# The last expert layer of a two-layer decoder: the branch behind the gathers' issue, the last norm on VectorE, the second bias in the residual, the plain norms in one group

## Chip, core and metric

One NeuronCore of a Trainium2 chip. The metric is the device time of one execution of the whole program, in microseconds (us), as the median of several runs. TensorE is called PE, VectorE DVE, ScalarE ACT, GpSimd POOL and SyncE SP, as in the profile. PE multiplies into PSUM, DVE and ACT work elementwise, POOL does small elementwise work and issues the indirect DMAs (gathers and scatters), SP issues plain DMAs.

## What is computed

The reference is a decoder of two layers over 8 sequences of 256 tokens of 256 numbers. Each layer is attention, cross attention and a mixture of experts, each followed by a residual and a layer norm. The change touches the end of the second layer: its cross attention's last block, and its experts.

```
x = layernorm(x + cross_attention(x, ctx))            # second layer
probs = softmax(x @ gate_w.T)                         # 2048 tokens, 8 experts
top2_w, top2_idx = top_k(probs, 2)
keep = counts <= cap                                  # cap = 1.25 * 2048 / 8 = 320
h = silu(x_of_expert @ w1[e] + b1[e])
y = h @ w2[e] + b2[e]
out = layernorm(x + sum over kept experts of y * probability)
```

An expert that got more than 320 assignments is dropped as a whole. With the given data at most two experts are kept, and the kernel handles one kept expert by a short way; for more than two (a number the program reads at run time) a branch runs a general way, `all_experts`. In all runs here the branch is not entered: its body is jumped over.

## The kernel before

Activations live in SBUF as `x`, 16 chunks of 128 tokens; two chunks are a block `b`, 0 to 7. The order of PE, ACT, DVE and POOL is written out by hand: each stage is a list of steps with block offsets (`round_of`), and `run` records them. Only SP, and POOL in the expert stage, are ordered by the scheduler.

**Second cross attention (`xattn`, L657 to L791).** In round b the steps run for blocks around b: scores, weights, averages for b, projection and residual for b-1 (`settle`, L611), then the norm of b-2 (`norm`, L126: two ACT instructions), its transpose (`turn_batch`), its rows to DRAM for the later gathers (`store`, L967), router logits and ranking (`logits`, `rank`). Tokens that no kept expert takes need only the final norm of x itself: `plain` (L1192) takes moments of a block on DVE and POOL, `give` (L1196) normalizes it on ACT into a buffer, and SP sends it to `out`. In the rounds `plain` runs three blocks behind and `give` four. After the last round a second list (L774) finishes blocks 6 and 7.

`moments` (L110) is: two `bn_stats` and two `bn_aggr` on DVE, then on POOL (L120 to L123) variance plus epsilon, power -0.5, minus the mean, times the scale. The norm is then one ACT instruction per chunk with scale and bias.

**Experts (`ffn1`, L1423).** In this order:
1. `choose` (L1097): counts against the cap, the `first` kept expert, and two whole numbers `n` (which expert, how many).
2. `values_load` (L1435): every engine loads the count into a register, then `tc.If(n > 2)` (L1436): every engine branches over `all_experts`.
3. `slots` (L1116): DVE and PE work out the tokens of the expert in 3 slots of 128 (`tok`).
4. three gathers `own` of token rows (L1442, by `gather` L1222), POOL.
5. `weigh` (L1177): the tokens' probabilities, transposed on PE, copied by ACT, stored to DRAM by SP; three gathers `wts` from there (L1446).
6. PE loads the expert's number (L1447). Per slot one PSUM tile `sums[i]` with two halves; PE puts the biases b1 and b2 into them by products with a row of ones (L1453: six matmuls, twelve rows in the trace).
7. `plain` of blocks 6 and 7; the rows are transposed (`turned`, L1469, copied out by DVE), first product (L1461), SiLU on ACT (L1484), `give` of blocks 6 and 7 (four ACT instructions), transposes of h (copied out by ACT, L1471), second product (L1461).
8. Per slot (L1497 to L1501): y = second sum times weight plus own row, moments on DVE, rsqrt on POOL; then, in a second loop, the norm on DVE (L1505) and the scatter to `out` (L1506), which waits for all blocks' stores, since it overwrites rows of them.

Of the kernel before, what the change touches and what calls it, by code (L numbers as in the profile page):

```python
# [10 lines left out]
F32 = mybir.dt.float32  # L11
# [7 lines left out]
P = 128  # L19
# [23 lines left out]
def decoder_kernel(ctx: ExitStack, tc: tile.TileContext, a, out):  # L43
# [66 lines left out]
    def moments(b, y):  # L110

        st = small.tile([P, 2, 6], F32, tag="st2", name="st2")
        mv = small.tile([P, 2, 2], F32, tag="mv2", name="mv2")
        rs = small.tile([P, 2], F32, tag="rs2", name="rs2")
        nm = small.tile([P, 2], F32, tag="nm2", name="nm2")
        for c in range(2):
            nc.vector.bn_stats(st[:, c, :], y[:, c, :])
        for c in range(2):
            nc.vector.bn_aggr(mv[:, c, :], st[:, c, :])  # L119
        nc.gpsimd.tensor_scalar(rs, mv[:, :, 1], EPS, None, ALU.add)  # L120
        nc.gpsimd.tensor_tensor(rs, rs, mhalf[:, 0:2], ALU.pow)
        nc.gpsimd.tensor_scalar(nm, mv[:, :, 0], -1.0, None, ALU.mult)
        nc.gpsimd.tensor_tensor(nm, nm, rs, ALU.mult)  # L123
        waiting[b] = y, rs, nm

    def norm(b):  # L126
# [382 lines left out]
    class Steps:  # L509
# [101 lines left out]
        def settle(self, b):  # L611
            add_residual(b, self.py.pop(b), self.y.pop(b), self.bk)


    def xcontext(w, ctxT, es):
# [41 lines left out]
    def xattn(w, given, clamp, route, es):  # L657
# [50 lines left out]
        if clamp is None:  # L708
# [57 lines left out]
            (store, -2),  # L766
            (give, -4),
            (st.residual, 0),
# [3 lines left out]
            (rank, -2),  # L772
            (plain, -3),
        ], [  # L774
            (st.turn, B - 1),
            (st.project, B - 1),
            (st.settle, B - 1),
            (norm, B - 2),
            (turn_batch, B - 2),
            (store, B - 2),  # L780
            (logits, B - 2),
            (norm, B - 1),
            (turn_batch, B - 1),
            (store, B - 1),
            (give, B - 4),
            (rank, B - 2),
            (plain, B - 3),
            (logits, B - 1),
            (give, B - 3),
            (rank, B - 1),  # L790
# [136 lines left out]
    class Route:  # L927
# [169 lines left out]
        def choose(self):  # L1097


            p = ps.tile([P, 512], F32, tag="ps", name="p_cnt")  # L1100
            mm(p[:, 0:NE], [(onesb, self.acc[:, NC, :])])
            keep = self.keep = self.kept([NE], "keep")
            first = self.first = self.kept([NE], "first")
            prior = self.temp([NE, NE], "prior")
            n = self.temp([2], "n")
            self.n = self.kept([2], "ni", I32)
            nc.vector.tensor_scalar(keep, p[:, 0:NE], float(CAP), None, ALU.is_le)
            nc.vector.tensor_tensor(prior, tri, keep.unsqueeze(1).broadcast_to([P, NE, NE]), ALU.mult)
            nc.vector.tensor_reduce(first, prior, AX.X, ALU.add)
            nc.vector.scalar_tensor_tensor(first, first, 0.0, keep, ALU.is_equal, ALU.mult)  # L1110
            nc.vector.tensor_tensor(prior[:, 0, :], first, iota[:, 0:NE], ALU.mult)
            nc.vector.tensor_scalar(prior[:, 1, :], keep, 1.0 / NE, None, ALU.add)
            nc.vector.tensor_reduce(n, prior[:, 0:2, :], AX.X, ALU.add)
            nc.vector.tensor_copy(self.n, n)

        def slots(self):  # L1116
# [33 lines left out]
            for h in range(2):  # L1150
                oh = self.temp([NC // 2, P], "oh", BF16)
                shape = [P, NC // 2, P]
                nc.vector.tensor_tensor(  # L1153
                    oh, iotab.unsqueeze(1).broadcast_to(shape),
                    row[:, h * (NC // 2):(h + 1) * (NC // 2)].unsqueeze(2).broadcast_to(shape), ALU.is_equal,
                )
                for c in range(NC // 2):
                    nc.tensor.matmul(  # L1158
                        p[:, 0:2 * NS], oh[:, c, :], o2[:, h * (NC // 2) + c].rearrange("p i n -> p (i n)"),
                        start=(h + c == 0), stop=(h == 1 and c == NC // 2 - 1),  # L1160
                    )
            at = self.temp([NS], "at")
            tok = self.kept([NS], "tok", I32)
# [3 lines left out]

            to = self.kept([NS], "to", I32)
            none = self.temp([NS], "none")
# [4 lines left out]

            return tok, to, places

# [246 lines left out]
    def ffn1(r, b1, b2, b1r, w1, w2, ys, dump):  # L1423

        rows = r.rows.rearrange("c k p d -> (c k p) d")
        with ExitStack() as es:
# [7 lines left out]
            nc.scalar.activation(unused, r.lg[:, NC - 1, 0:1], AF.Silu)  # L1434
            n = nc.values_load(r.n[0:1, 1:2], min_val=1, max_val=NE)  # L1435
            with tc.If(n > 2):  # L1436
                all_experts(r, b1, b2, w1, w2, ys, dump, rows)
            tok, to, places = r.slots()
            own, wts = [], []
            for i in range(NS):  # L1440
                own.append(wk.tile([P, D], F32, tag="own", name="own"))
                gather(own[i], rows, tok[:, i:i + 1])  # L1442
            wrows = r.weigh()
            for i in range(NS):
                wts.append(wk.tile([P, 1], F32, tag="wts", name="wts"))
                gather(wts[i], wrows, tok[:, i:i + 1])  # L1446
            e = nc.tensor.value_load(r.n[0:1, 0:1], min_val=0, max_val=NE - 1)  # L1447

            sums = []
            for i in range(NS):  # L1450
                p = ps.tile([P, 2, D], F32, tag="ps", name="p_u")
                for k, b in ((0, b1r), (1, b2.rearrange("p e d -> p (e d)"))):
                    nc.tensor.matmul(  # L1453
                        p[:, k, :], ones[0:1, :], b[0:1, bass.ds(e * D, D)],
                        start=(k == 0), stop=False, skip_group_check=True,
                    )
                sums.append(p)

# [7 lines left out]
            def turned(t, name):  # L1466
                pt = ps.tile([P, 512], F32, tag="ps", name="pt_" + name)
                for f in range(2):
                    nc.tensor.transpose(pt[:, f * P:(f + 1) * P], t[:, f * P:(f + 1) * P], ident)  # L1469
                tT = wk.tile([P, 2, P], F32, tag=name + "T", name=name + "T")  # L1470
                (nc.scalar.copy if name == "h" else nc.vector.tensor_copy)(  # L1471
                    tT, pt[:, 0:2 * P].rearrange("p (k t) -> p k t", k=2)
                )
                return tT

            f1, f2 = (w.rearrange("p e c n -> p (e c n)") for w in (w1, w2))
            for b in range(B - 2, B):
                r.plain(b)
            xgT = [turned(own[i], "xg") for i in range(NS)]
            hs = []  # L1480
            for i in range(NS):
                into(0, i, xgT[i], f1)
                hs.append(wk.tile([P, D], F32, tag="h", name="h"))
                nc.scalar.activation(hs[i], sums[i][:, 0, :], AF.Silu)  # L1484
            for b in range(B - 2, B):
                r.give(b)
            hT = [turned(hs[i], "h") for i in range(NS)]
            for i in range(NS):
                into(1, i, hT[i], f2)
            places()  # L1490
            ends = []
            for i in range(NS):
                y = wk.tile([P, D], F32, tag="y1", name="y1")
                st = small.tile([P, 6], F32, tag="st1", name="st1")
                mv = small.tile([P, 2], F32, tag="mv1", name="mv1")
                rs = small.tile([P, 1], F32, tag="rs1", name="rs1")
                nc.vector.scalar_tensor_tensor(y, sums[i][:, 1, :], wts[i][:, 0:1], own[i], ALU.mult, ALU.add)  # L1497
                nc.vector.bn_stats(st, y)  # L1498
                nc.vector.bn_aggr(mv, st)
                nc.gpsimd.tensor_scalar(rs, mv[:, 1:2], EPS, None, ALU.add)  # L1500
                nc.gpsimd.tensor_tensor(rs, rs, mhalf[:, 0:1], ALU.pow)  # L1501
                ends.append((y, mv, rs))
            fixed = []
            for i, (y, mv, rs) in enumerate(ends):
                nc.vector.tensor_scalar(y, y, mv[:, 0:1], rs, ALU.subtract, ALU.mult)  # L1505
                s = nc.gpsimd.indirect_dma_start(  # L1506
                    out=out, out_offset=bass.IndirectOffsetOnAxis(ap=to[:, i:i + 1], axis=0), in_=y, in_offset=None,
                    bounds_check=NT - 1, oob_is_err=False,
                )
                after(s, r.given)  # L1510
                for other in fixed:
                    tc.declare_no_dep(s.ins, other.ins, reason="no two slots have one token")
                fixed.append(s)

    def after(s, others):
# [7 lines left out]
    def all_experts(r, b1, b2, w1, w2, ys, dump, rows):  # L1523

        with ExitStack() as es:
# [31 lines left out]
            for e in range(NE):  # L1557
                xg = wk.tile([P, 2, NS * P], F32, tag="xgT", name="xgT")
                for i in range(NS):
# [7 lines left out]
                    )  # L1567
                hT = wk.tile([P, 2, NS * P], F32, tag="hT", name="hT")
                for f in range(2):
# [9 lines left out]
            for b in range(B):  # L1579
                z = wk.tile([P, 4, D], F32, tag="z", name="z")  # L1580
                load_back(z, returned(ys, 2)[b], sent)
# [8 lines left out]
                nc.gpsimd.tensor_copy(x[:, 2 * b:2 * b + 2, :], y)  # L1590
            nc.vector.memset(r.first, 0.0)
            for b in range(B - 2):
                r.plain(b)
# [214 lines left out]
```

## Time and profile before

| what | value |
|---|---|
| runs | 1028.88, 1022.90, 1025.72 us; median 1025.72 |
| profiled execution | 1028.25 us; its span from first to last instruction 1026.5 us |
| mean granted PE clock | 0.952 of full |
| busy over the span | PE 927.8, DVE 568.3, ACT 494.4, POOL 296.0 us |

Busy time by stretch of the span (us), with the granted clock:

| stretch | PE | DVE | ACT | POOL | PE clock |
|---|---|---|---|---|---|
| 800 to 850 | 42.98 | 23.11 | 23.87 | 16.04 | 0.97 |
| 850 to 900 | 44.27 | 32.06 | 28.90 | 4.04 | 1.00 |
| 900 to 950 | 42.01 | 36.93 | 30.07 | 11.11 | 0.89 |
| 950 to 984 | 17.18 | 16.51 | 10.00 | 5.40 | 0.55 |
| 984 to 1027 | 18.52 | 13.54 | 4.17 | 14.17 | 0.58 |

How to read it: up to about 950 us PE works nearly without a gap. After that no engine is busy for more than about half of the time: the last block's chain and the experts' chain run from engine to engine, and what counts there is which wait ends last. In the views, a time is the start from the span's beginning and the next number the duration; a name such as `DVEq` is the engine's sequencer, which handles loads of registers, branches and waits.

### The profile page before, as it was taken

To read this page: it belongs to the slowest core of one execution; us is meant where nothing else is said; L and a number is where in the kernel's file an instruction comes from. 1 tells how busy PE (TensorE), PEld (TensorE's weight loads), DVE (VectorE), ACT (ScalarE), POOL (GpSimd) and SP (SyncE) were. 2 spreads that over 40 slices of the span, in tenths; PEclk is the share of its full clock that TensorE was granted. 3 is DMA by queue.
4 is the path that set the end of the run, shared out by engine and by line. 5 is a ranking of instruction groups with operands and counts; after the bars stand their busy time and mean duration, and the time that the engine had idled before them with its cause. 6 is when DMAs were issued, how large, how long until landed. Compare 5 with 4: busy or idle time off the path is not lost. (4 is left out here: it accounts for less than half of the span.)

```text
span 1026.5 us, 24279 instructions
## 1 busy us (share of the span) xinstructions
PE 927.8 (90%) x9877; PEld 623.3 (61%) x9877; DVE 568.3 (55%) x1480; ACT 494.4 (48%) x1055; POOL 296.0 (29%) x533
## 2 busy tenths in 40 slices
PE   8999999998999859999999999999999978888633
PEld 4677767765677546666666645666666556665522
DVE  3987776784577752222222246666665445776551
ACT  5677777745666422212222135555565545556211
POOL 3232222241211322333332133344433520112222
PEclk9999999999999969999999999999999999998556
DMA  8100000007211271222111030000000041001110
GB/s 233 14 3 3 3 3 3 3 10 267 75 42 43 56 225 49 67 67 66 58 42 42 21 113 22 22 22 1 2 1 1 2 158 59 15 29 42 39 32 29
DMA packets 45367, 50.97 MB, mean 50 GB/s; under 512 B 9854, under 2 KB 37806, under 8 KB 45249
## 3 DMA queue, kind: packets, MB, share of 16 engines
q1 hardware_dynamic: 37170, 36.37, 10.9%
q0 software_dynamic: 4256, 10.87, 3.7%
q10 hardware_dynamic: 3824, 2.10, 0.8%
q8 instruction: 82, 1.34, 0.6%
q14 instruction: 35, 0.29, 0.1%
HBM read 36.00 MB, written 13.51 MB: 48 GB/s over the span
## 5 line engine op out<-in xcount | busy, mean ns | idle before, releaser
L120 POOL TENSOR_SCALAR rs<-mv 128x2 f32<-128x2 f32 x48 | 15.2, 316 | 337.9 <-DVE mv L119 200.3
L852 DVE TENSOR_REDUCE m<-p_s 128x2 f32<-128x512 f32 x128 | 78.7, 683 | 50.2 <-PE p_s L846 50.2
L1382 DVE TENSOR_TENSOR h<-h,p_v 128x512 f32<-128x512 f32 x36 | 24.8, 688 | 109.6 <-PE p_v L1376 109.6
L870 ACT ACTIVATE e<-p_st 128x512 f32<-128x512 f32 x128 | 66.3, 618 | 30.0 <-PE p_st L553 30.0
L54 PE MATMUL p_pv<-e,vals 77*32 77x256 f32 (+1 forms) x1024 | 70.6, 396 | 11.3 <-DVE e L696 10.4
L1391 ACT COPY hT<-pt_h 128x512 f32<-128x512 f32 x36 | 21.1, 586 | 118.8 <-PE pt_h L1389 118.8
L689 ACT ACTIVATE e<-p_st 77x512 f32<-77x512 f32 x128 | 65.3, 591 | 21.7 <-PE p_st L553 21.7
L1228 POOL DMA_INDIRECT ys<-yo,dst x36 | 35.4, 985 | 135.6 <-DVE yo L1403 135.6
L1398 PE MATMUL p_y<-fw,hT 128*128 x288 | 68.1, 379 | 0.7 <-ACT hT L1391 0.7
L1398 PEld LDWEIGHTS p_y<-fw,hT 128*128 128x128 f32 x288 | 54.6, 190 | 23.3 <-issue 16.5
L1376 PE MATMUL p_u<-fw,xgT 128*128 x144 | 67.9, 594 | 0.4 <-DVE d L1347 0.4
L1376 PE MATMUL p_v<-fw,xgT 128*128 x144 | 67.7, 592 | 0.0
L873 POOL TENSOR_SCALAR_AFFINE_SELECT e<-e 128x256 f32<-128x256 f32 x128 | 49.9, 407 | 36.3 <-ACT e L870 31.9
L673 DVE TENSOR_REDUCE m<-p_s 128x4 f32<-128x308 f32 x128 | 52.1, 469 | 12.6 <-PE p_s L54 12.0
L54 PEld LDWEIGHTS p_pv<-e,vals 77*32 77x32 f32 (+1 forms) x1024 | 33.3, 111 | 38.4 <-issue 8.0
L562 ACT COPY u<-p_pv 128x512 f32<-128x512 f32 x48 | 28.2, 588 | 55.4 <-PE p_pv L54 55.3
L1376 PEld LDWEIGHTS p_v<-fw,xgT 128*128 128x128 f32 x144 | 27.4, 190 | 34.4 <-issue 34.4
L129 ACT ACTIVATE x<-y,nm,rs 128x256 f32<-128x256 f32 x64 | 34.9, 597 | 24.3 <-POOL nm L123 24.3
L1381 ACT ACTIVATE h<-p_u 128x512 f32<-128x512 f32 x36 | 21.5, 597 | 46.0 <-PE p_u L1376 36.5
L1222 POOL DMA_INDIRECT xg<-rows,tok x36 | 35.1, 975 | 28.8 <-DMA fw<-in_L_ffn_W 15.7
L863 PE MATMUL p_st<-qT,kT 32*128 32x256 f32 x512 | 41.9, 400 | 0.0
L375 POOL COPY aT<-s 32x128 f32<-32x128 f32 x32 | 9.3, 289 | 104.6 <-DVE s L371 103.9
(304 smaller groups left out, 2137.2 us busy)
## 6 DMA issues: line engine op xcount, KB each, us to landing
fw<-in_L_ffn_W SPq DMA_DIRECT2D x24, 512.0 KB, 6.7
rows<-x SPq DMA_DIRECT2D x24, 256.0 KB, 2.2
z<-ys SPq DMA_DIRECT2D x8, 512.0 KB, 3.8
m<-in_L_ffn_w SPq DMA_DIRECT2D x16, 256.0 KB, 5.1
x<-in_x SPq DMA_DIRECT2D x8, 256.0 KB, 7.8
out<-plain SPq DMA_DIRECT2D x8, 256.0 KB, 2.1
b<-in_L_ffn_b SPq DMA_DIRECT2D x8, 128.0 KB, 4.8
xg<-rows,tok POOLq DMA_INDIRECT x36, 2.8
```

The source lines that it names most:

```text
L54: nc.tensor.matmul(dst, l, r, start=(i == 0), stop=(i == n - 1))
L129: nc.scalar.activation(x[:, 2 * b + c, :], y[:, c, :], AF.Identity, bias=nm[:, c:c + 1], scale=rs[:, c:c + 1])
L673: nc.vector.tensor_reduce(st.less(b)[:, c, j, :], p, AX.X, ALU.max, negate=True)
L689: nc.scalar.activation(e[0:KV, i].rearrange("p i q -> p (i q)"), p[0:KV].rearrange("p i q -> p (i q)"), AF.Exp)
L852: nc.vector.tensor_reduce(st.less(b)[:, c, j, 2 * t:2 * t + 2], p, AX.X, ALU.max, negate=True)
L863: nc.tensor.matmul(tiles[j][:, i, :], kTs[b][r, t, i, c * P:(c + 1) * P], st.qT[b][r, t, :], start=(i == 0), stop=False, skip_group_check= ...
L870: nc.scalar.activation(e.rearrange("p i q -> p (i q)"), p.rearrange("p i q -> p (i q)"), AF.Exp)
L873: nc.gpsimd.affine_select(out=e[:, :, o], in_=e[:, :, o], compare_op=ALU.is_ge, fill=0.0, base=0, pattern=[[0, 2], [2 * c - 1, P]], channe ...
L1222: nc.gpsimd.indirect_dma_start(out=out, out_offset=None, in_=table, in_offset=bass.IndirectOffsetOnAxis(ap=index, axis=0),)
L1228: s = nc.gpsimd.indirect_dma_start(out=table, out_offset=bass.IndirectOffsetOnAxis(ap=index, axis=0), in_=rows, in_offset=None,)
L1376: nc.tensor.matmul(p, xg[:, dc, :], w[:, bass.ds(e * (2 * FF) + dc * FF, FF)], start=(dc == 0), stop=(dc == 1),)
L1398: nc.tensor.matmul(y, hT[:, f * P:(f + 1) * P], w3[:, bass.ds(e * (4 * D) + f * D, D)], start=(f == 0), stop=(f == 3),)
```

## The change

Seven things, all near the end:
- The last block's residual takes its moments at once (`settle_now`, with the new `statistics`), and its norm is done by DVE (`norm_now`) with the mean subtracted and the scale multiplied, so POOL has only the power left to do.
- In the rounds `plain` runs four blocks behind and `give` five; blocks 4 to 7 are left to the expert stage, where `statistics` takes the eight chunks' moments in one group.
- `values_load` and the branch stand behind the issue of all gathers, not ahead of `slots`. The two numbers are worked out in `numbers`, inside `slots`.
- Only b1 is put in by products. b2 is added to the own row on DVE (`own_b`), times the weight, ahead of the end.
- Blocks 4 to 7 are normalized one by one, block 4 on ACT, the others on DVE, each sent by a DMA of its own from four buffers.
- The copies of the transposed own rows go from DVE to ACT.
- At the end slots are interleaved: end(0), end(1), send(0), end(2), send(1), send(2). Variance plus epsilon is DVE's, the power POOL's.

In the jumped-over body, two tiles get fewer buffers, `at` is set to -1, and the statistics are taken again.

```diff
+    def statistics(y, pool, tag):
+        n = y.shape[1]
...
+        for c in range(n):
+            nc.vector.bn_stats(st[:, c, :], y[:, c, :])
+        for c in range(n):
+            nc.vector.bn_aggr(mv[:, c, :], st[:, c, :])
+        nc.vector.tensor_scalar(rs, mv[:, :, 1], EPS, None, ALU.add)
+        nc.gpsimd.tensor_tensor(rs, rs, mhalf[:, 0:1].broadcast_to([P, n]), ALU.pow)
+        return mv, rs
...
+        def settle_now(self, b):
+            y = self.bk.tile([P, 2, D], F32, tag="y2", name="y2")
+            nc.vector.tensor_tensor(y, self.py.pop(b), self.y.pop(b), ALU.add)
+            self.y[b] = y, *statistics(y, self.bk, "n")
+
+        def norm_now(self, b):
+            y, mv, rs = self.y.pop(b)
+            for c in range(2):
+                nc.vector.tensor_scalar(
+                    x[:, 2 * b + c, :], y[:, c, :], mv[:, c, 0:1], rs[:, c:c + 1], ALU.subtract, ALU.mult
+                )
...
-            (give, -4),
+            (give, -5),
...
-            (plain, -3),
+            (plain, -4),
         ], [
...
-            (st.settle, B - 1),
+            (st.settle_now, B - 1),
...
-            (norm, B - 1),
+            (st.norm_now, B - 1),
...
-            (give, B - 4),
             (rank, B - 2),
-            (plain, B - 3),
+            (give, B - 5),
             (logits, B - 1),
-            (give, B - 3),
             (rank, B - 1),
...
         def choose(self):
...
-            nc.vector.tensor_tensor(prior[:, 0, :], first, iota[:, 0:NE], ALU.mult)
-            nc.vector.tensor_scalar(prior[:, 1, :], keep, 1.0 / NE, None, ALU.add)
-            nc.vector.tensor_reduce(n, prior[:, 0:2, :], AX.X, ALU.add)
+        def numbers(self):
...
+            nc.vector.tensor_tensor(at[:, 0, :], self.first, iota[:, 0:NE], ALU.mult)
+            nc.vector.tensor_scalar(at[:, 1, :], self.keep, 1.0 / NE, None, ALU.add)
+            nc.vector.tensor_reduce(n, at, AX.X, ALU.add)
             nc.vector.tensor_copy(self.n, n)
...
+            self.numbers()
             at = self.temp([NS], "at")
...
-            n = nc.values_load(r.n[0:1, 1:2], min_val=1, max_val=NE)
-            with tc.If(n > 2):
-                all_experts(r, b1, b2, w1, w2, ys, dump, rows)
-            tok, to, places = r.slots()
+            tok, at, places = r.slots()
...
             wrows = r.weigh()
+            last = slice(2 * B - 8, 2 * B)
+            mv, rs = statistics(x[:, last, :], wk, "p")
             for i in range(NS):
                 wts.append(wk.tile([P, 1], F32, tag="wts", name="wts"))
                 gather(wts[i], wrows, tok[:, i:i + 1])
+            n = nc.values_load(r.n[0:1, 1:2], min_val=1, max_val=NE)
+            with tc.If(n > 2):
+                all_experts(r, b1, b2, w1, w2, ys, dump, rows)
...
+            places()
             e = nc.tensor.value_load(r.n[0:1, 0:1], min_val=0, max_val=NE - 1)
...
-                for k, b in ((0, b1r), (1, b2.rearrange("p e d -> p (e d)"))):
-                    nc.tensor.matmul(
-                        p[:, k, :], ones[0:1, :], b[0:1, bass.ds(e * D, D)],
-                        start=(k == 0), stop=False, skip_group_check=True,
-                    )
+                nc.tensor.matmul(
+                    p[:, 0, :], ones[0:1, :], b1r[0:1, bass.ds(e * D, D)], start=True, stop=False,
+                    skip_group_check=True,
+                )
...
+            def give(b, eng):
+                o = wk.tile([P, 2, D], F32, tag="plain", name="plain", bufs=4)
...
-                (nc.scalar.copy if name == "h" else nc.vector.tensor_copy)(
+                nc.scalar.copy(
...
-            for b in range(B - 2, B):
-                r.give(b)
+            for b in range(B - 4, B):
+                give(b, nc.scalar if b < B - 3 else nc.vector)
             hT = [turned(hs[i], "h") for i in range(NS)]
...
+            ev = nc.vector.value_load(r.n[0:1, 0:1], min_val=0, max_val=NE - 1)
             for i in range(NS):
...
+                nc.vector.scalar_tensor_tensor(
+                    t, b2.rearrange("p e d -> p (e d)")[:, bass.ds(ev * D, D)], wts[i][:, 0:1], own[i],
+                    ALU.mult, ALU.add,
+                )
+                own_b.append(t)
+            def end(i):
...
+                nc.vector.scalar_tensor_tensor(
+                    y[:, 0, :], sums[i][:, 1, :], wts[i][:, 0:1], own_b[i], ALU.mult, ALU.add
+                )
+                ends.append((y, *statistics(y, small, "e")))
+            def send(i):
...
+            for i in range(NS + 1):
+                if i < NS:
+                    end(i)
+                if i:
+                    send(i - 1)
```

## The prediction

> **What bounds the kernel now.** First the table by stretches: to 950 us PE is busy 42 to 44 of every 50 us, and the change puts nothing on PE there. So I read the last 75 us: the timeline, then the chain of work that ended last, then the rows of the branch's line. (Columns: start, duration.) The timeline of the last block's norm:
>
> ```profile
> 963.15 0.69 DVE L136 TENSOR_TENSOR y<-p_y,x 128x512 f32<-128x512 f32 x1 [1.65 <-PE p_y L54]
> ...
> 968.59 0.23 POOL L120 TENSOR_SCALAR rs<-mv 128x2 f32<-128x2 f32 x1
> 968.91 0.71 POOL L121 TENSOR_TENSOR rs<-rs,mhalf 128x2 f32<-128x2 f32 x1
> ...
> 970.22 1.09 ACT L129 ACTIVATE x<-y,nm,rs 128x256 f32<-128x256 f32 x2 [2.41 <-POOL nm L123]
> ...
> 974.64 0.17 DVE L985 TENSOR_REDUCE sm<-p_l 128x2 f32<-128x16 f32 x1 [3.25 <-PE p_l L54]
> ```
>
> To see: the residual is ready at 963.84, x only at 971.31. Between them DVE does a plain block's moments first and POOL that block's four small operations, so this block's start at 968.59. PE, DVE and ACT wait.
>
> The branch's line (ns min/median/max, first and last start):
>
> ```profile
> L1436 DVEq COMPARE_BRANCH  x1: 56/56/56, 980.3 to 980.3; - x1
> L1436 PEldq COMPARE_BRANCH  x1: 3583/3583/3583, 980.3 to 980.3; - x1
> L1436 POOLq INC_SWDGE_SEM  x1: 1797/1797/1797, 981.2 to 981.2; - x1
> L1436 DVEq EVENT_SEMAPHORE  x1: 21/21/21, 984.2 to 984.2; - x1
> ```
>
> To see: PE and DVE need 3.6 and 3.9 us to get over the jumped body; ACT and POOL get on at 980.7. And the chain behind it:
>
> ```profile
> 984.27 0.29 DVE own L1121
> ...
> 992.47 5.45 PE p_u L1453 x12
> 997.92 1.47 PE pt_xg L1469 x6
> 999.39 4.84 PE p_u L1461 x12
> ...
> 1005.03 0.59 ACT plain L1200
> ...
> 1006.11 0.49 ACT plain L1200
> ...
> 1006.91 3.58 PE p_u L1461 x8
> ...
> 1014.50 0.71 POOL out L1506
> ...
> 1017.20 0.97 POOL out L1506
> ```
>
> To see: bias products, transposes, first product, two blocks' norms on ACT in the way of hT, second product, and three scatters in a row. From the last scatter's start to the span's end are 9.3 us that the change doesn't touch.
>
> **The change, part by part**, all in times of this profile.
>
> *Last norm.* In the changed program's order DVE does, from the residual's end at 963.84, the rest of the previous ranking mixed with this block's moments: 0.41, 0.39, 0.42, 0.39, 0.18, twice 0.16, 0.19, 0.18 = 2.5 us, so epsilon is in at 966.3. POOL has the power alone (0.71, L121) and nothing ahead of it: 967.1. DVE norms the first chunk (0.4, as L1505), then one addition (0.19), two bn_stats of a plain block (0.74), one aggregate (0.16), then the second chunk (0.4): 969.0 against 971.31. **Gain 2.3.** What is late next: the previous blocks' ranking on DVE (967.84 to 970.52, 2.7 us) now runs 969.15 to 971.85, and the logits arrive at 974.64 - 2.3 = 972.3, so 0.5 us of cover. Ends: 0 (that cover gone and POOL slowed), 3.1 (the eight logit products take 1.06 us at 964.22 under clock 1.00, 1.88 at 972.73 under 0.50, if the shorter gap keeps the clock). I take 2.3, the direct sum.
>
> *Branch and second bias.* `first` ends at 979.15, and `slots` starts there instead of 984.27: 5.1 us earlier. The four instructions of `numbers` (0.66, L1111 to L1114) stand ahead of `at`, where DVE waited 0.47 for PE: 0.2 lost. So `tok` is there at 985.7, the own gathers go at 986.5, 987.9 and 989.1 (spacing 1.3 as before, the same 0.8 after `tok`), the last landing 3.2 us later (gathers' median), 992.3.
> But the branch now stands behind `statistics` on DVE: ws done at 986.5, eight bn_stats (0.37 each, L117 0.74 for two) and eight aggregates (0.15 each) = 4.2, epsilon 0.2: 990.7. Then 4.3 from the register's load to the event behind the jump (979.9 to 984.2): **995.0**. PE meets its own branch at 987.0, and 0.3 + 3.6 + 0.6 (load of the expert's number, 991.6 to 992.2) bring it to 991.5. There it stops: in the built program its first bias product (L1489 of the changed kernel) waits for a DVE count that lies past DVE's branch, since the jumped body uses the same PSUM buffers. Queued behind it are all products, and everything waits for those. From 995.0 three bias matmuls at 5.45/6 = 0.9 each end at 997.7, against 997.92. **Gain 0.2**: 5.1 + 2.7 us shorter work, of which DVE's 4.4 us of statistics and the later jump eat nearly all. Ends: gain 3.6 if DVE's jump costs nothing (PE from 991.5, end 994.3, the gathers there by 992.3); loss 1.0 if the jump's code comes 1.2 us later. I take 0.2, since DVE jumps over some 240 instructions where 230 cost 3.9.
> [...]
>
> *Elsewhere in that stage, at no cost.* POOL: power over eight columns, between 0.58 (one column) and 2.8 (four times two columns' 0.71), about 1.5; it delays the last weight gather to about 994.4, landing by 997; POOL leaves the branch after that and after 1.8 of INC_SWDGE_SEM, at 999, needed at 1009. DVE behind the jump: places 0.4, two nm 0.4, six norms 2.4, a register load 0.3, three own_b at 0.5: done by about 1001, needed at 1007.6. SP: four stores at 0.38; two stand in the queue behind the one that waits for ACT's block, so they go by 1006.9 and land at about 1009 (2.1 each), where the first scatter waits for them at 1011.4: cover 2.4, and without it what is over is lost. The copies of xg on ACT take 0.30 (L1471) for DVE's 0.43, hidden by PE's own transposes.
>
> *Plain norms on ACT.* Between h and hT stand two instructions instead of four, 2.06/4 = 0.51 each. **Gain 1.0**; ends 0.5 (a wait for the transposes instead, ending 1005.1) and 1.1.
>
> *End.* Second product shifted by 0.2 + 1.0: slot 0's y at 1007.6. Its residual 0.48, stats 0.43, aggregate 0.18, epsilon 0.17, with hand-offs 1009.0; power 0.58: 1009.7. Slot 1's row of four ends at 1010.7, then norm 0: 1011.0; POOL's second power 1011.36; first scatter 1011.45 (1.10). Slot 2 ends at 1012.4, but its power stands behind that scatter: 1012.85 to 1013.45. Second scatter 1013.5, third 1014.8 against 1017.20: 2.4, of which 1.2 are the shift. **Gain 1.2.** Ends 0 (POOL's gaps of 0.3 at each change) and 2.0 (no power between the scatters).
>
> *Rounds.* Each round keeps one plain and one give, one block later; the moved blocks' 1.1 us of ACT and 1.0 of DVE each leave a stage that PE bounds: 0, ends -0.5 and +1.0.
>
> Sum: 2.3 + 0.2 + 1.0 + 1.2 = 4.7. Against the profiled execution's own 1028.25 that is 1023.6. That execution is 2.5 above the median of the runs, so against the median of 1025.72: **1021.0**.
>
> **Rivals.**
> - *B, DVE's jump doesn't hold PE.* For: ACT's and POOL's jumps cost 0.4, and both fetches lay at one time before. Against: the 3.9 row. 3.4 more: 1017.6. Chance 0.10.
> - *C, the clock stays up.* In the rows by microsecond the granted clock is 0.50 from 997 to 1003, 1.00 from 1004 to 1007, 0.58 at 1007 and 0.50 to 1010, after the gap of 1005.1 to 1006.9. That gap shrinks by 1.0. At the factor 1.88/1.06 the second product's 4.54 would take 2.6: 2 more, 1019.0. Against: first product and bias may as well fall on other steps of the clock. Chance 0.12. [...]
> - *D, the norm's gain isn't there*: DVE's mixed order makes ranking late, or POOL's power is slowed by DVE. 1023.3. Chance 0.17.
> - *E, slower*: DVE's fetch at 991 now runs among the six gathers' packets (before, DMA moved little but instructions at 979 to 985, and 27 to 261 GB/s at 993 to 997), and nothing else covers it. Every us more is one of span; from 3.9 + 4.7 = 8.6 us on it is slower than before. At three times, 11.7: 1028.8. Against: the busy share of DMA at 993 to 997 is 0.25 to 0.47. Chance 0.06, mostly with a smaller loss.
> - The forecast itself: 0.55, alone 1018.8 to 1023.3.
>
> **The numbers.** A measurement tells about 0.5% (5.1 us) from no change. 1020.6 is that bound, close under the forecast: of the forecast 0.40 falls beyond, of B and C nearly all, of D none: 0.22 + 0.20 = 0.42 faster. Slower by over 0.5% is about half of E and a little for what I don't see: 0.05. The rest, 0.53, is within. The range runs from B's side, 1017.0, to D with the worse ends of the stores and of POOL's gaps, 1024.8; the runs' own spread of 1022.9 to 1028.88 is part of that.
>
> **What would show it.** Right: the last x normed by DVE about 2 us sooner; DVE's event behind the branch about 4 us after the load, PE's first bias product straight behind it; bias, transposes and products ending no more than some 0.3 us sooner counted from `first`; two ACT norms ahead of hT; scatters 1.3 to 2.1 apart. Wrong: PE's bias products before DVE's event; scatters waiting for the blocks' stores; a fetch of over 6 us.

## The result, and the profile after

The changed kernel takes 1016.16 us (median of 5 runs, 1014.33 to 1018.12); the kernel before, beside it, 1027.66 (5 runs): ratio 0.9895, 95% interval 0.9863 to 0.9927. A second set of runs gave 1017.41 (6 runs) against 1025.35 (19 runs): 0.9918, interval 0.9888 to 0.9948. Over all eleven runs the changed kernel's median is 1016.68; the kernel before has 1024.64 to 1025.35 in its four larger sets (12 to 22 runs). So the gain is **some 8.4 us (8.0 to 8.7), where 4.7 was forecast**: faster, as the forecast says, but by nearly twice as much, and the 1016.16 lies below the forecast's range (1017.0 to 1024.8).

The profiled execution (1016.16, span 1014.4) is 12.1 us shorter than that of before. About 3 of these are the first profile's bad luck: at 1028.25 it lay some 3 above the median of its kernel.

The last block's norm, in the timeline (start, duration):

```profile
959.04 0.69 DVE L631 TENSOR_TENSOR y<-p_y,x 128x512 f32<-128x512 f32 x1 [1.17 <-PE p_y L54]
...
960.64 0.42 DVE L133 BATCH_NORM_STATS2 st<-y 128x6 f32<-128x256 f32 x1
960.97 0.17 DVE L1039 TENSOR_SCALAR sel<-rk 128x32 bf16<-128x32 f32 x1
961.04 0.24 DVE L135 BATCH_NORM_AGGREGATE mv<-st 128x2 f32<-128x6 f32 x2
...
961.32 0.17 DVE L136 TENSOR_SCALAR rs<-mv 128x2 f32<-128x2 f32 x1
961.57 0.71 POOL L137 TENSOR_TENSOR rs<-rs,mhalf 128x2 f32<-128x2 f32 x1 [9.39 <-DVE rs L136]
...
963.46 0.38 DVE L637 TENSOR_SCALAR x<-y,mv,rs 128x256 f32<-128x256 f32 x1
...
967.17 0.18 DVE L1010 TENSOR_REDUCE sm<-p_l 128x2 f32<-128x16 f32 x1 [0.65 <-PE p_l L54]
```

To see: x is ready 4.11 after the residual's end (959.73 to 963.84), where it was 7.47. On DVE the second bn_stats is given as 0.42, but the next instruction starts 0.33 later, and the two aggregates together take 0.24.

The branch's line (ns min/median/max, first and last start):

```profile
L1477 PEldq COMPARE_BRANCH  x1: 3356/3356/3356, 979.4 to 979.4; - x1
...
L1477 DVEq COMPARE_BRANCH  x1: 56/56/56, 982.4 to 982.4; - x1
L1477 PEldq EVENT_SEMAPHORE  x1: 51/51/51, 982.8 to 982.8; - x1
...
L1477 DVEq EVENT_SEMAPHORE  x1: 21/21/21, 986.3 to 986.3; - x1
```

To see: PE is over the body at 982.8, DVE 3.9 after its own branch at 986.3. DVE branches later than PE because the statistics of eight chunks stand ahead: 2.70 for eight bn_stats from 978.75 on, 0.62 for eight aggregates from 981.37 on. The chain of waits (start, duration) goes on behind DVE's event:

```profile
986.60 2.90 PE p_u L1489 x6
...
995.51 1.08 ACT plain L1506 x2
...
996.90 1.15 PE p_u L1515 x4
...
1001.91 0.49 POOL out L1562
```

To see: PE's bias products start 0.3 behind DVE's event; one block's two norms stand ahead of hT. The three scatters start at 1001.91, 1003.75 and 1005.09.

### The profile page after: what moved, and what is told of

The parts are those of the page before. It is cut to its first block, busy times and chain, and to the rows that moved or that the text cites. A ratio compares the mean times of both kernels' runs of the same rounds, so it can differ in the third digit from the quotient of the medians.

```text
span 1014.4 us, 24247 instructions
## 1 busy us (share of the span) xinstructions
PE 919.8 (91%) x9871; PEld 617.2 (61%) x9871; DVE 571.0 (56%) x1495; ACT 491.2 (48%) x1050; POOL 289.0 (28%) x512
## 5 line engine op out<-in xcount | busy, mean ns | idle before, releaser
L54 PE MATMUL p_pv<-e,vals 77*32 77x256 f32 (+1 forms) x1024 | 68.0, 384 | 10.7 <-DVE e L723 9.8
```

The source lines that it names most:

```text
L54: nc.tensor.matmul(dst, l, r, start=(i == 0), stop=(i == n - 1))
```

## The experiments

Besides the first runs of the two kernels, twelve more were made: ten variants, and each of the two kernels once more. The sets have 5 to 12 runs of each kernel, whose single times spread over 3.6 to 8 us (the kernel before, with up to 22 runs beside them, over up to 11.7); so a difference of 2 us between two medians is a trend, and the profiles' stretches carry the explanation. The table gives them (us between starts): A, from the third block's residual of the second cross attention to the fourth's; B, the next; C, last residual but one to last residual; D, last residual to the last logits' reduction; E, end of `first` to the transposes of the gathered rows; F, from those to the second product; G, second product to third scatter. From the third scatter to the end it is 9.3 to 9.4 in all.

| kernel | median us | A | B | C | D | E | F | G |
|---|---|---|---|---|---|---|---|---|
| before | 1025.18 | 15.95 | 15.13 | 13.29 | 11.49 | 18.70 | 9.06 | 10.29 |
| before_again | 1025.04 | 15.96 | 16.02 | 10.61 | 11.49 | 18.71 | 7.70 | 9.03 |
| norm_alone | 1022.96 | 15.95 | 14.47 | 10.20 | 8.27 | 18.56 | 8.14 | 9.03 |
| rounds_undone | 1018.45 | 15.96 | 15.13 | 13.32 | 8.28 | 15.66 | 7.81 | 8.40 |
| norm_undone | 1019.27 | 15.21 | 14.46 | 12.11 | 11.48 | 17.73 | 6.75 | 8.19 |
| after | 1016.16 | 15.21 | 14.46 | 10.28 | 8.13 | 17.74 | 7.48 | 8.19 |
| after_again | 1017.41 | 15.20 | 14.46 | 12.10 | 8.13 | 17.67 | 6.75 | 8.19 |
| statistics_behind | 1015.93 | 15.21 | 14.45 | 10.13 | 8.13 | 15.55 | 7.93 | 8.63 |
| statistics_split | 1016.03 | 15.20 | 14.45 | 12.10 | 9.90 | 15.21 | 7.10 | 8.31 |
| b2_products | 1019.97 | 15.21 | 14.45 | 12.11 | 8.13 | 20.36 | 7.41 | 8.32 |
| branch_ahead | 1015.53 | 15.20 | 14.45 | 13.36 | 8.13 | 15.80 | 8.97 | 8.18 |
| statistics_early | 1014.51 | 15.21 | 14.47 | 10.70 | 8.14 | 15.47 | 6.49 | 8.19 |
| plain_behind | 1015.49 | 15.20 | 14.46 | 9.33 | 8.14 | 15.82 | 6.96 | 8.29 |
| ends_apart | 1018.77 | 15.20 | 14.47 | 10.81 | 8.13 | 17.37 | 7.02 | 8.94 |

Three theories went in. 1: the gain is the parts' own work, mis-sized. 2: the 4.1 us by which the first profile of the changed kernel is ahead at the last residual already come from the rounds' shift. 3: those 4.1 are chance, from the steps of PE's granted clock.

**The norm alone.** `(st.settle, B - 1)` and `(norm, B - 1)` of the kernel before become:

```diff
+            (st.settle_now, B - 1),
...
+            (st.norm_now, B - 1),
```

> The kernel before, with only the last block's norm changed (residual with its own moments, norm on VectorE). From the last residual's start to the logits' reduction the kernel before took 11.49 us and the changed one 8.13. Theory 1, the norm's own work: 8.1 to 9.2 here, and a whole 2.3 (the forecast's sum) to 3.4 us faster than before, with the residual itself where it was (963.2). Theory 2, the 4.1 us ahead of the residual come from the rounds' shift: the residual stays at 963, since the shift isn't in this kernel. Theory 3, they are steps of PE's granted clock that fall by chance: the residual lies anywhere between 959 and 963.5.

D is 8.27, and the median 2.2 below before's, a little under the 2.3 to 3.4 expected (ratio 0.9976, 0.9956 to 0.9996): theory 1 for the norm. C is 10.20 with the old rounds: C is no gain of the shift.

**The norm undone** in the changed kernel.

```diff
-            (st.settle_now, B - 1),
+            (st.settle, B - 1),
...
-            (st.norm_now, B - 1),
+            (norm, B - 1),
```

> The changed kernel with the last block's norm done the old way (moments partly on POOL, norm on ACT). Theory 1: 11.5 us from the last residual to the logits' reduction instead of 8.13, and 2.3 to 3.4 us slower than the changed kernel as a whole. Rival (the ranking of the blocks before is what ends last, so the norm's gain is not on the path): no change. Theory 2: the residual itself starts at 959 as in the changed kernel. Theory 3: anywhere between 959 and 963.5.

D is 11.48, and the median 2.6 above the changed kernel's 1016.68: the 3.35 of the row are on the path. C of 12.11 with the new rounds speaks for theory 3.

**The rounds undone.**

```diff
-            (give, -5),
+            (give, -4),
...
-            (plain, -4),
+            (plain, -3),
...
-            last = slice(2 * B - 8, 2 * B)
+            last = slice(2 * B - 4, 2 * B)
```

> The changed kernel with the rounds' offsets as before (plain three blocks behind, give four), so the expert stage has two blocks left instead of four and its statistics are of four chunks. Theory 2 (the shift took plain work out of the last rounds' path): the last residual at 963 instead of 959, 4 us lost, of which DVE's shorter statistics (four bn_stats and four aggregates less, 1.7 us in the changed kernel's rows) give back about 1.7 by an earlier branch: 2.4 slower. Theory 3 (clock by chance): the residual between 959 and 963.5 whatever the offsets, and the whole about 1.7 us faster, as PE gets past DVE's branch 1.7 earlier. The forecast on record (the shift costs nothing) says the same as theory 3 for the whole.

By medians it was 1.8 slower than 1016.68 (the ratios' intervals overlap), though E is 2.1 shorter: the shift looks worth something after all, and neither theory has it whole. C swings from 10.20 to 13.32 with the old offsets and from 9.33 to 13.36 with the new. But A is 15.95 or 15.96 in four of four kernels with the old offsets, and 15.20 or 15.21 in ten of ten with the new. The timelines of before and after show why:

```profile
899.79 0.74 DVE L117 BATCH_NORM_STATS2 st<-x 128x6 f32<-128x256 f32 x2
900.45 0.30 DVE L119 BATCH_NORM_AGGREGATE mv<-st 128x2 f32<-128x6 f32 x2
900.67 1.19 DVE L696 TENSOR_SCALAR e<-e 77x2048 f32<-77x2048 f32 x1
...
902.00 1.07 PE L54 MATMUL p_pv<-e,vals 77*32 77x256 f32 x16 [0.78 <-DVE e L696]
```

```profile
898.33 0.76 DVE L1041 TENSOR_TENSOR acc<-acc,sel 128x8 bf16<-128x8 bf16 x4
899.00 1.22 DVE L723 TENSOR_SCALAR e<-e 77x2048 f32<-77x2048 f32 x1
...
900.37 1.07 PE L54 MATMUL p_pv<-e,vals 77*32 77x256 f32 x16
```

To see: in this round of before, plain's moments stand on DVE ahead of the clipping of e, and PE waits 0.78 for it; in the changed kernel plain has not begun in this round, and this wait is gone (a later one, for the next clipping, is in both: 0.87 and 0.97). And the tables by stretches (columns: length, then busy time of PE, PEld, DVE, ACT, POOL; PE's granted clock third from the end) of before, then after:

```profile
902.00:905.00 3.00, 2.13 (x36) 1.25 (x40) 3.00 (x7) 0.59 (x1) 1.13 (x3) 0.96 0.00 0
905.00:908.00 3.00, 3.00 (x22) 1.94 (x15) 2.79 (x10) 0.92 (x2) 0.00 (x0) 0.50 0.02 5
```

```profile
902.00:905.00 3.00, 2.03 (x30) 1.33 (x23) 2.91 (x7) 0.82 (x3) 0.00 (x0) 1.00 0.03 5
905.00:908.00 3.00, 2.58 (x19) 2.02 (x17) 2.85 (x11) 1.66 (x4) 0.58 (x2) 1.00 0.00 0
```

DVE is the full engine there (3.00 and 2.91 of 3), and PE at 2.13 isn't. In before a window at half clock (0.50 from 905 to 908) follows PE's gap; with the old offsets this is so in three profiles of four, with the new ones in none of ten. B is 15.13, 16.02, 14.47 (the one without a slow window) and 15.13 with the old offsets (mean 15.19), 14.45 to 14.47 in all ten others. Together the shift is worth 0.75 + 0.73 = 1.5; the 0.73 is a mean over four profiles, and that the gap brings the slow window was not tested apart.

**The statistics behind the branch** on DVE.

```diff
-            last = slice(2 * B - 8, 2 * B)
-            mv, rs = statistics(x[:, last, :], wk, "p")
...
             places()
+            last = slice(2 * B - 8, 2 * B)
+            mv, rs = statistics(x[:, last, :], wk, "p")
```

> The changed kernel with the eight chunks' statistics behind the branch instead of ahead of it on DVE. Theory (DVE's jump holds PE's first bias product): DVE's event behind the branch comes some 3.7 us sooner, at about 982.5 against 986.3, PE is then held by its own jump alone (982.8), the first bias product starts at about 983.2 instead of 986.6, and the whole is 2.5 to 3.5 us faster than the changed kernel. Rival (PE is held by something else, such as its own jump or the gathers' landing): bias products at 986.6 as before, no change. Second rival: the statistics, now behind, end last for ACT's plain block or for the stores, and 1 us or more of the gain is lost at the end.

```profile
L1475 DVEq EVENT_SEMAPHORE  x1: 21/21/21, 981.6 to 981.6; - x1
L1475 PEldq EVENT_SEMAPHORE  x1: 51/51/51, 982.6 to 982.6; - x1
...
983.73 2.89 PE L1486 MATMUL p_u<-b1r,ones 1*128 x6 [5.06 <-DVE st L133]
```

To see: DVE's event came ahead of PE's own, and the bias products at 983.73, 1.1 behind PE's event; E fell by 2.2. So DVE's jump does hold PE in the changed kernel. The whole gained less than the runs can tell: the weight gathers had gone behind the branch on POOL, with the power and ACT's block behind them.

```profile
987.72 0.94 POOL L1251 DMA_INDIRECT wts<-wrows,tok  x1 [5.97 <-DMA ys<-yo,dst]
...
991.17 1.69 POOL L137 TENSOR_TENSOR rs<-rs,mhalf 128x8 f32<-128x8 f32 x1
...
993.09 1.09 ACT L1503 ACTIVATE plain<-x,nm,rs 128x256 f32<-128x256 f32 x2 [0.75 <-DVE nm L1502]
```

To see: gathers 987.72 (983.40 in the changed kernel), power behind the last of them, ACT's block behind the power, and hT behind that, at 994.08. This is my second rival in its effect, but not in its cause: the statistics were done at 985.44, and ACT's block waited for POOL.

**The changed kernel again.**

> The changed kernel once more, unchanged. It asks how much of one profiled execution is chance. Theory 3 (steps of PE's granted clock, 3.41 us long, fall by chance on the last rounds): the stretch from the last residual but one to the last residual, 10.28 in the changed kernel's first profile and 10.1 to 13.3 in the five others so far, can come out anywhere in that range, and the times of single runs spread over some 4 us. From the last residual to the logits 8.1 to 8.3 and from first to the transposes of the gathered rows 17.7 as before, whatever the clock. Rival (the 10.28 belongs to the changed kernel): 10.3 again.

C is 12.10 and F 6.75, so both move between two executions of one program, as theory 3 has it. D and G repeat to 0.01, E to 0.07.

**The statistics split**, with `early_statistics` taking `statistics(x[:, 2 * B - 8:2 * B - 4, :], ...)`.

```diff
+            (early_statistics, 0),
             (logits, B - 2),
             (st.norm_now, B - 1),
...
-            last = slice(2 * B - 8, 2 * B)
+            last = slice(2 * B - 4, 2 * B)
```

> The changed kernel with the statistics of blocks 4 and 5 taken in the last list, between two uses of DVE where it waits for PE, so that only four chunks' statistics stand ahead of the branch. Theory (DVE's later jump holds PE, the rest of the hold is PE's own jump): the stretch from first to the transposes of the gathered rows falls from 17.74 to 15.6, as it did in the two kernels with fewer or no statistics ahead of the branch (15.66 and 15.55), and as POOL's weight gathers stay ahead of its branch, nothing is late at the end: 2.0 us faster than the changed kernel, 1014.2. Rival (the gain is given back at the end, as with the statistics behind the branch): the same as the changed kernel within 0.5 us.

E is 15.21 as expected, but D is 9.90, so 1016.03 as a whole: the early statistics ran on DVE in the middle of the last norm.

```profile
961.96 0.71 POOL L142 TENSOR_TENSOR rs<-rs,mhalf 128x2 f32<-128x2 f32 x1 [11.21 <-DVE rs L141]
...
962.19 0.42 DVE L138 BATCH_NORM_STATS2 st<-x 128x6 f32<-128x256 f32 x1
...
965.11 0.73 DVE L642 TENSOR_SCALAR x<-y,mv,rs 128x256 f32<-128x256 f32 x2
```

To see: the power is in at 962.67, x starts at 965.11.

**The second bias by products again.**

```diff
...
+                for k, b in ((0, b1r), (1, b2.rearrange("p e d -> p (e d)"))):
+                    nc.tensor.matmul(
+                        p[:, k, :], ones[0:1, :], b[0:1, bass.ds(e * D, D)],
...
-                    y[:, 0, :], sums[i][:, 1, :], wts[i][:, 0:1], own_b[i], ALU.mult, ALU.add
+                    y[:, 0, :], sums[i][:, 1, :], wts[i][:, 0:1], own[i], ALU.mult, ALU.add
```

> The changed kernel with the second bias put in by products again (six bias matmuls instead of three) and no own_b on DVE. Theory of the forecast: three more one-row products at 5.45/6 = 0.9 us each stand between DVE's event and the transposes of the gathered rows: that stretch 2.7 longer (20.4 from first instead of 17.74), 2.7 us slower as a whole. Rival (the products run while something else is waited for): no change. Of the clock: if one-row products don't bring the granted clock up, the step to full clock comes one window (3.4 us) later too, and the second product may fall before it: another 1 to 1.7 us.

E is 20.36, 2.65 more than the mean of both changed profiles, the first product starts later by as much (21.70 behind `first`, against 19.08 and 19.00), and the median is 2.6 above after_again: the forecast's 2.7. The second product kept its full clock (2.85 us, 2.86 in the changed kernel).

**The branch ahead of the slots again.**

```diff
+            r.numbers()
+            n = nc.values_load(r.n[0:1, 1:2], min_val=1, max_val=NE)
+            with tc.If(n > 2):
...
             tok, at, places = r.slots()
...
-            n = nc.values_load(r.n[0:1, 1:2], min_val=1, max_val=NE)
-            with tc.If(n > 2):
...
```

> The changed kernel with the branch, and the numbers it needs, ahead of the slots again; the statistics stay where the changed kernel has them. Theory: DVE and PE jump at one time (5.1 us between first and the slots), and then nothing holds PE's bias products, which can run while the gathers are under way: from first to the transposes 5.1 more for the jump, less the hold. By rows: slots at 5.1 after first instead of 0, gathers 7.1 later as in both kernels, third landing some 3.2 after its issue, so transposes at 5.1 + 7.1 + 2.7 + 0.5 = 15.4 to 16.3 from first, against 17.74: 1.5 to 2.3 us FASTER than the changed kernel. Rival (the branch's new place is what gained, as the forecast's 5.1 says): slower by 1 us or more.

E is 15.80, as expected: up to the first slot's transposes, moving the branch costs 1.9 us.

```profile
L1465 DVEq COMPARE_BRANCH  x1: 56/56/56, 977.4 to 977.4; - x1
L1465 PEldq COMPARE_BRANCH  x1: 3680/3680/3680, 977.4 to 977.4; - x1
...
L1465 DVEq EVENT_SEMAPHORE  x1: 21/21/21, 980.9 to 980.9; - x1
```

To see: both jumps at one time, where in the changed kernel they lie one behind the other (979.4 and 982.4). But E ends too early to tell what this is worth:

```profile
994.68 0.69 PE L1520 MATMUL pt_xg<-ident,own 128*128 128x128 f32 x2 [1.23 <-DMA own<-rows,tok]
...
995.16 1.06 PE L1512 MATMUL p_u<-m,xgT 128*128 x2
```

To see: the third slot's transposes wait for the third gather, issued at 990.77 and landing 3.9 later, and the first product stands behind them. It starts 18.92 behind `first` (995.16, and 976.24); in the changed kernel 19.08 (990.76, and 971.68), where this gather landed at 985.4 and DVE's jump ends last. So **moving the branch costs 1.9 us at the transposes, but less than 0.2 at the first product**: with the branch ahead another wait takes the place of the jump. My expectation adds the third gather's issue and leaves its landing out. F of 8.97 holds that wait. The whole is 1.9 faster than after_again by medians (0.9905 against 0.9918), but the intervals overlap, and the profile shows no cause for it: from `first` to the third scatter it takes 32.95, between the 33.41 and 32.61 of the changed kernel's two profiles.

**The kernel before again.**

> The kernel before once more, unchanged, for how much of its first profile was chance. Fixed by the work, as in its first profile and in the kernels with its rounds: 15.95 from the third block's residual to the fourth's (15.20 in all seven kernels with the shifted rounds), 11.5 from the last residual to the logits, 18.6 from first to the transposes of the gathered rows, 0.3 + 9.0 from the last scatter to the end. By chance of the granted clock's 3.41 us windows: 14.47 or 15.13 for the next block (15.13 where the PE gap at 900 to 905 makes a window slow), 10.2 to 13.4 for the last residual, 9.0 or 10.3 from the second product to the last scatter, depending on whether the window behind the ACT norms is slow. Rival (the first profile is typical): 13.3 and 10.3 again, span about 1026.

C is 10.61, F 7.70, G 9.03: the rival falls, the first profile was a bad draw in all three. B is 16.02, more than either value that I named. Its second product took 2.86 us, as in the changed kernel, where the first profile had 4.54:

```profile
1005.22 2.86 PE L1461 MATMUL p_u<-m,hT 128*128 x12 [1.77 <-ACT hT L1471]
```

**The statistics early**: as in the split, but at the head of the last list.

```diff
+            (early_statistics, 0),
             (st.turn, B - 1),
             (st.project, B - 1),
...
```

> The changed kernel with the statistics of blocks 4 and 5 at the head of the last list, so that they run on DVE ahead of the last two residuals, where it sat idle for 2.65 us, and not beside the last block's norm (where, in the kernel with the split statistics, they took 1.77 us of the norm's gain). Theory: last residual to logits 8.13 again, first to transposes 15.2 (17.7 in the changed kernel): 2.5 us faster than the changed kernel, 1014.4 against its 1016.9 over both sets of runs. Rival (the last rounds are bound by DVE where I put them): the round of the last residual but one gets up to 1.2 longer, gain 1.3.

D 8.14, E 15.47, median 1014.51, ratio 0.9902 (0.9879 to 0.9924): as expected, 2.2 below the changed kernel by medians, though the intervals overlap. What it costs in the round in which it now stands is 0.4 at most: 16.35 from the fifth to the sixth block's residual, against 15.95 to 16.21 in the kernels without them.

**ACT's plain block behind hT**, on top of that.

```diff
-            for b in range(B - 4, B):
-                give(b, nc.scalar if b < B - 3 else nc.vector)
+            for b in range(B - 3, B):
+                give(b, nc.vector)
             hT = [turned(hs[i], "h") for i in range(NS)]
+            give(B - 4, nc.scalar)
```

> The kernel with the early statistics, and ACT's plain block behind the copies of hT instead of ahead of them. Theory (hT waits behind two norms of 0.54 on ACT): from the transposes of the gathered rows to the second product 0.5 to 0.9 less than in the kernel with the early statistics at the same step of the clock, so 0.5 to 0.9 us faster, about 1013.7. Rival (hT waits for the transposes of h, or ACT's block, now later, makes its store the last that the first scatter waits for): the same or slower.

F is 6.96 with the step to full clock late, 5.4 us behind the transposes; by the line found below, the kernel with ACT's block ahead would have 7.8 at that step: 0.8 gained. The whole, 1015.49, shows nothing of it; the six runs spread over 5 us.

**The ends apart.**

```diff
-            for i in range(NS + 1):
-                if i < NS:
-                    end(i)
-                if i:
-                    send(i - 1)
+            for i in range(NS):
+                end(i)
+            for i in range(NS):
+                send(i)
```

> The changed kernel with the three slots' ends in two loops again (residual and moments of all three, then norms and scatters). Theory: the third scatter is bound by DVE's work and POOL's three powers and scatters either way; from the second product to the third scatter 8.2 to 8.6 against 8.19: no more than 0.4 slower. The forecast's term for the end (1.2, most of it from the interleaving and from one power instead of two small operations on POOL): if it were the interleaving, 1 us slower.

My expectation fell: G is 8.94, 0.75 more; with DVE's third residual and moments ahead of the first norm, the first scatter comes 6.29 behind the second product (1001.07, and 994.78), in the changed kernel 5.01 (1001.91, and 996.90). The interleaving is worth 0.75 in this stretch. The median is 2.1 above 1016.68, more than that; the six runs spread over 5.9 us.

## Why the prediction was wrong, step by step

The four parts that were forecast to gain did gain, and on the path that the prediction names. Two of them, the norm and the branch, were sized too small, and one term, the rounds, was put at nothing for a reason that doesn't hold.

- **Last norm, forecast 2.3, measured 3.35** (D). The mechanism and the order are as forecast; the size is off, and beyond the upper end of 3.1. I added the durations of DVE's instructions: 2.5 from the residual's end to epsilon. It took 1.76 (959.73 to 961.49), since the next instruction starts before the one ahead has ended (bn_stats 0.41 long, 0.33 apart; eight aggregates in 0.62, not 1.2). That is 0.7 of the missing 1.05; the rest lies behind the power in the same way (two norms and what stands between them in 1.53, not 1.9). The overlap is some 0.08 us both for a bn_stats of 0.41 and for an aggregate of 0.15 (eight of each take 2.70 and 0.62); that it is a fixed part of each instruction is an estimate of mine from these two. The ranking of the blocks before wasn't late; rival D falls.
- **Branch and second bias, forecast 0.2, measured 1.0** (E, 18.70 to 17.7; at the first product 20.04 to 19.0). PE stops at DVE's count past the branch, as forecast (DVE's event at 986.3, PE's first bias product at 986.60); rival B falls, and E too, with DVE's jump at 3.9. The statistics were shorter (DVE's load 3.2 behind the last of `ws`, not 4.2), again by overlap; this is the term that was mis-sized. (The sum itself is 0.2 off: 986.5 + 4.2 + 0.2 is 990.9, not 990.7.) Taken apart with the branch behind: b2 gives 2.65 (forecast 2.7). The branch's new place loses 1.9 at the transposes and less than 0.2 at the first product. The two can't be added at the first product: with the branch ahead, the b2 products make only some 1.1 there (20.04 behind `first` in before, which has them, 18.92 in branch_ahead), since the third gather's landing then comes last. That a jump's time is a fetch of code, as rivals B and E call it, is not shown: in before, of the jump from 980.3 to 984.2, the DMA view has five packets of instructions in 981 to 982 (four on q14, one on q8) and none from there to 984.
- **Plain norms, forecast 1.0, measured 1.0** at like clock. F depends on when the granted clock steps up: 6.49, 6.75, 7.02, 7.10, 7.41, 7.48, 7.81 where the step comes 2.7, 3.2, 3.8, 3.9, 4.6, 4.7, 5.4 behind the start of the transposes, 0.5 us for each us (without statistics_behind and plain_behind, in which ACT's block was late or moved, and branch_ahead, in which the transposes wait for a gather; after_again repeats the 6.75 at 3.3). The three profiles with the old tail have 7.70, 8.14, 9.06 at 3.2, 4.1, 5.9: 1.0 above that line each.
- **End, forecast 1.2, measured 0.84** (9.03 to 8.19, both with the second product at full clock); 0.75 are the interleaving. Rival C's state, the second product at full clock, came in the changed kernel's first profile, but not by the change: the kernel before has it too in before_again, and so has norm_alone, with the old tail.
- **Rounds, forecast 0 (ends -0.5 and +1.0), measured 1.5.** This is the step that failed as reasoning: "each leave a stage that PE bounds". I read that from stretches of 50 us; in the stretch of 902 to 905 DVE is busy 3.00 of 3 and PE 2.13, and PE waits 0.78 for DVE.

Sum: 3.35 + 1.0 + 1.0 + 0.84 + 1.5 = 7.7 of 8.4. The 0.7 left isn't settled. From the third to the last residual the four profiles with the old offsets take 70.8 us on average and the ten with the new ones 68.4, so 2.3 and not only 1.5; but single profiles range from 69.3 to 72.1 and from 66.7 to 70.8, and what exceeds the 1.5 lies in stretches such as C, which moves by up to 4 from execution to execution. No cause of it in the change is shown. Of theory 2, 1.5 of the 4.1 us hold; the rest fits theory 3, and 0.8 of the 4.1 were there before the second layer's first round (first residual at 862.23 and 861.43).

## What to carry to other kernels

Add DVE's work by the spacing of starts, not by durations (here 0.33 against 0.41 us for a bn_stats). Before an edit is called free because another engine bounds the stage, look at the few microseconds in which it stands: one DVE step of 1 us ahead of a clip cost 0.75 in the round, and in three of four profiles a window at half clock came behind it. Where a branch over a long body stands behind other work, look at which engine is over it last: here DVE branched 3.0 behind PE (982.4 and 979.4) and was over at 986.3, PE at 982.8, and PE's bias products waited for DVE. Whether that costs anything is read at the next point where all inputs meet: here 1.9 us at the transposes were less than 0.2 at the first product, since the gathers' landing stood next. Before explaining a difference of two profiles, profile each kernel twice.

## What the hardware showed that I had not expected

- In these profiles PE's granted clock stepped on a grid of 3.41 us (in before at 962.80, 966.21, 1003.76, 1007.17, 1010.58 and 1014.00, in the changed kernel at 956.60, 960.01 and 963.42) whose phase differed between executions: in the two profiles of the changed kernel the last residual starts at 959.04 and 962.92, and the step next to it comes at 960.01 and 962.36, once behind it and once ahead. Two profiles of one program differ by 2.7 us in C (13.29 and 10.61) and by 1.3 in G.
- Windows filled with one-row bias products don't seem to have brought the clock up: in before, bias from 992.47 to 997.92, full clock only at 1003.76; in b2_products, bias from 987.7 to 993.1, full clock at 997.64. In all fourteen profiles the step comes 2.7 to 5.9 us behind the first transpose. No kernel tested that by itself, so the cause stays open.
